# Surplus rows carried into the next table, earlier keys of pairs, and pairs at every second group in a graph-convolution kernel

## The chip, the core and the metric

The kernel runs on one core of a Trainium2 chip, in one launch. The metric is the device time of one execution in microseconds (us), taken over several runs. The core has five engines that work side by side: TensorE (PE, matmuls), VectorE (DVE), ScalarE (ACT), GpSimd (POOL) and SyncE (SP, which here only issues transfers).

## The reference

```python
h = jnp.maximum(_layernorm(x, axis=-1), 0.0)            # x: 12500 nodes x 128
h = h @ W_in2f.T
Wij = smu(f_ij @ W_f1.T + b_f1) @ W_f2.T + b_f2         # f_ij: 400000 edges x 20
Wij = Wij * rcut_ij[:, None]
x_ij = h[idx_j] * Wij                                    # idx_j sorted, idx_i random
agg = jax.ops.segment_sum(x_ij, idx_i, num_segments=12500)
out = x + smu(agg @ W_o1.T + b_o1) @ W_o2.T + b_o2
```

Per edge, a filter of 128 numbers is made from 20 features, multiplied with a row of `h` and added to the row of the edge's source node. The edges lie in the order of `idx_j`, so the rows of `h` are near each other, but the sums go to random nodes. That is what the kernel is built around.

## The kernel before, in words

Edges are worked on in tiles of 128, in groups of 4 tiles (`GRP`) and in sups of 2 groups; there are 3125 tiles, 782 groups and 391 sups. The nodes fall into 98 bins of 128. Each group makes its messages (edges on partitions, 128 numbers and the node's place in its bin: a row of 129 numbers, `ROW`), and POOL scatters them by an indirect transfer into a table in DRAM that has `CAP` slots for each bin. One scatter sends one row from each of 128 partitions, so a group needs four.

The sups are split into ten epochs (`PARTS`; called stages in the prediction). The messages of epoch k are scattered into table k (three stores, taken in turn), and while epoch k+1 is worked on, the table of epoch k is read back (`fetch`, on SP), DVE makes for each tile of 128 rows a selection matrix from the places (`choose`, tile `se`), and PE adds the tile to its bin's sum by a matmul (`add`). A table of 768 slots per bin is 6 tiles per bin, so 588 matmuls. A place carries a mark of its round, so that old rows in a store don't match. Stores that are used for the first time are cleared by transfers of a zero tile (`clear`), spread over the groups of the epoch before.

Which slot a row gets is worked out beforehand: DVE marks the bins of a sup (`mark_bins`), keeps running counts per bin (`bins`), PE makes prefix sums of the marks (`count`), DVE takes each row's slot from PSUM (`read`) and adds the bin's start (`number`).

In some groups rows are paired. In such a group rows of tiles 0 and 1 are matched with rows of tiles 2 and 3 that go to the same bin (`spread_keys`, `match`), rows that found a partner are moved beside it by permuting matmuls (`rank_left`, `place_left`, `permute`, `take_pairs`), and two scatters send two rows from each partition. The rows that found none are collected in one tile of leftovers (`lt`, at most 112 rows), which is counted and scattered with a later group, its host. A pair therefore needs 2 + 1 scatters in place of 4. `EVERY` says after how many groups another one is paired.

The order of the work on PE, DVE, ACT and SP is written out by hand: at step p the loop sends the messages of group p (those of a paired group one step later), numbers, weighs and mixes group p+1, counts and reads group p+2, and marks the bins of group p+3; the sums (`parts`) are spread evenly over an epoch's steps. The 23 sups of the last two epochs are worked early, one after every eight others in epochs 1 to 4; their messages are kept in DRAM and scattered at the end ("kept" groups). POOL's order follows from the calls of `scatter`.

## Time and profile before

| | |
|---|---|
| Time before, median of 3 runs | 3832.49 us (3823.35 to 3832.53) |
| The profiled execution's own time | 3826.85 us |
| Its span, first to last instruction | 3825.1 us |
| Mean granted TensorE clock | 0.964 of full speed |
| Busy share: PE, DVE, ACT, POOL | 86%, 81%, 74%, 75% |
| First and last scatter begin at | 12.99 and 3763.56 us |

The busy share counts the time in which an engine executes something. Time between two instructions in which it only takes up the next one does not count, and an engine can be at its limit with a share well below 100%. "issue" in a list of waits is such time.

### The profile page before, as it was taken

The page shows a single profiled execution, that of the slowest core. Times are in us where ns is not written, and L with a number is a line of the kernel's source. Part 1 is how long each engine was busy: PE and PEld are TensorE (multiplying, and loading weights), DVE is VectorE, ACT ScalarE, POOL GpSimd, SP SyncE. Part 2 cuts the span into 40 slices and gives each one's busy share as a digit, 9 for nine tenths or more (in the row PEclk, how much of TensorE's full clock was granted, in tenths as well). Part 3 has the DMA queues.
Part 4 walks back from the last instruction along what each step waited for, and adds up shares of the span by engine and source line. Part 5 has one row for each costly group of instructions (what it writes and reads, how often), then busy time and mean ns, then how long its engine had stood idle before and what let it go on. Part 6 is the DMA issues. An engine that isn't in the chain of part 4 may idle for free.

```text
span 3825.1 us, 90354 instructions
## 1 busy us (share of the span) xinstructions
PE 3294.2 (86%) x28066; PEld 2872.9 (75%) x28066; DVE 3116.8 (81%) x8275; ACT 2839.2 (74%) x7986; POOL 2855.5 (75%) x2946
## 2 busy tenths in 40 slices
PE   8777776988888999999989889999999889997767
PEld 4346665877777888878878778888888888887657
DVE  7878976877777888888888888888898888886657
ACT  7767766878888888888888888888778777875102
POOL 6777777777767777777777777777777777777776
PEclk9989988999999999999999999999999999999889
DMA  5888888888888878888878878888888888886977
GB/s 156 231 236 239 236 230 233 248 251 246 263 253 232 238 227 231 244 239 235 229 222 232 235 214 242 253 239 247 232 244 249 233 235 246 241 236 177 312 247 228
DMA packets 663936, 905.06 MB, mean 237 GB/s; under 512 B 179875, under 2 KB 462631, under 8 KB 663321
## 3 DMA queue, kind: packets, MB, share of 16 engines
q1 hardware_dynamic: 556025, 666.99, 63.5%
q0 software_dynamic: 100112, 219.93, 17.8%
q10 hardware_dynamic: 7312, 12.29, 0.9%
q8 instruction: 228, 3.74, 0.4%
q14 instruction: 259, 2.12, 0.2%
HBM read 500.66 MB, written 398.23 MB: 235 GB/s over the span
## 4 chain that ended last, share of the span: by engine, by line
PE 33%; DMA 18%; DVE 16%; ACT 11%; issue 11%; POOL 9%; SPq 2%; ACTq 0%; DVEq 0%; POOLq 0%
DMA buf<-ms,ix 12%; PE pg L1168 10%; POOL buf L1110 9%; PE pw L998 6%; PE pt L875 5%; ACT hg L973 3%; PE pc L752 3%; DVE se L1155 3%; DVE mt L838 2%; DVE ms L1040 2%; ACT oh L634 2%; ACT ge L926 2%; PE ph L954 2%; PE pw L1000 1%; DVE pc L796 1%
## 5 line engine op out<-in xcount | busy, mean ns | idle before, releaser
L1110 POOL DMA_INDIRECT buf<-ms,ix x2516 | 2444.3, 971 | 813.6 <-issue 569.0
L1168 PE MATMUL pg<-se,rw 128*128 128x128 f32 x8036 | 1168.7, 284 | 107.8 <-DVE se L1155 61.2
L1168 PEld LDWEIGHTS pg<-se,rw 128*128 128x128 f32 x8036 | 1037.2, 194 | 166.4 <-issue 65.5
L973 ACT ACTIVATE hg<-ph,w_sb 128x128 f32<-128x128 f32 x2784 | 781.9, 361 | 94.5 <-PE ph L954 80.4
L998 PE MATMUL pw<-w_f,ge 128*128 128x128 f32 x5568 | 779.2, 284 | 30.5 <-DVE ms L1040 14.3
L998 PEld LDWEIGHTS pw<-w_f,ge 128*128 128x128 f32 x5568 | 697.5, 197 | 50.0 <-issue 23.7
L1155 DVE TENSOR_TENSOR se<-irow_ps,rw 128x1536 f32<-128x1536 f32 (+1 forms) x345 | 587.4, 1703 | 112.1 <-DMA rw<-buf 89.5
L634 ACT ACTIVATE oh<-rbc,nrow 128x512 bf16<-128x512 uint8 x725 | 538.6, 743 | 33.5 <-DMA rbc<-rel_dram 33.1
L635 ACT ACTIVATE oh<-oh,onesb 128x512 bf16<-128x512 bf16 x743 | 536.0, 721 | 24.2
L796 DVE TENSOR_REDUCE pc<-pc 128x4 f32<-128x392 f32 (+1 forms) x782 | 466.4, 596 | 81.0 <-PE pc L752 77.4
L1040 DVE TENSOR_TENSOR ms<-pw,hg 128x512 f32<-128x512 f32 x482 | 330.2, 685 | 137.8 <-DMA buf<-ms,ix 36.5
L875 PE MATMUL pt<-ms,mt 128*128 128x129 f32 x2676 | 345.0, 279 | 55.0 <-DVE at L855 48.2
L875 PEld LDWEIGHTS pt<-ms,mt 128*128 128x128 f32 x2676 | 319.1, 193 | 66.7 <-issue 23.3
L752 PE MATMUL pc<-eo,tri 128*128 128x392 f16 x782 | 261.5, 334 | 69.8 <-DVE ix L818 46.8
L954 PE MATMUL ph<-hw,oh 126*128 126x128 bf16 x2784 | 274.4, 221 | 39.0 <-ACT hg L973 36.0
L926 ACT ACTIVATE ge<-pu 128x512 f32<-128x512 f32 x451 | 272.9, 605 | 17.4 <-PE pu L918 15.5
L752 PE MATMUL pc<-so,ones_h 128*128 128x392 f16 (+1 forms) x996 | 279.4, 306 | 0.1
L1000 PE MATMUL pw<-wls,f 128*128 128x128 bf16 x2784 | 274.2, 222 | 0.0
L1088 ACT ACTIVATE ms<-lo_b,mark 128x4 f32<-128x4 uint8 x309 | 91.3, 295 | 231.9 <-DVE ms L1040 219.7
L1110 POOL DMA_INDIRECT buf<-lt,ix x214 | 203.3, 950 | 78.0 <-issue 27.7
L954 PEld LDWEIGHTS <-oh 126*128 126x128 bf16 x2784 | 217.0, 99 | 52.5 <-issue 44.3
L752 PEld LDWEIGHTS <-ones_h 128*128 128x128 f16 x1554 | 151.8, 98 | 139.2 <-issue 17.1
(344 smaller groups left out, 5313.0 us busy)
## 6 DMA issues: line engine op xcount, KB each, us to landing
rw<-buf SPq DMA_DIRECT2D x292, 774.0 KB
f<-f_parts SPq DMA_DIRECT2D x370, 240.0 KB
buf<-zero SPq DMA_DIRECT2D x146, 387.0 KB
rbc<-rel_dram SPq DMA_DIRECT2D x389, 128.0 KB
buf<-ms,ix POOLq DMA_INDIRECT x2516
f_parts<-hs SPq DMA_DIRECT2D x105, 360.0 KB
rw<-buf SPq DMA_DIRECT2D x49, 645.0 KB
f_parts<-hs SPq DMA_DIRECT2D x107, 240.0 KB
```

Of the source, the lines that this page charges most:

```text
L634: nc.scalar.activation(oh, loaded[s][1][:, o:o + n], AF.Abs, bias=pneg if s < FEW // SUP else nrow)
L635: nc.scalar.activation(oh, oh, AF.Relu, scale=-1.0, bias=onesb[:, 0:1])
L752: nc.tensor.matmul(to, by, of, start=start, stop=stop, skip_group_check=True)
L796: nc.vector.tensor_reduce(sl[:, :n], pc[:, :n], op=ALU.max, axis=AX.X)
L875: nc.tensor.matmul(po[:, j * (ROW + 1):j * (ROW + 1) + w], pp[:, o:o + P], ms[:, i, ROW:ROW + w], start=(i == 0), stop=(i == 1))
L954: nc.tensor.matmul(ph[:, j * P:(j + 1) * P], oh[:3 * WIN, a:a + P], hw[:3 * WIN, g % PER, :], start=True, stop=True)
L973: nc.scalar.activation(hg[:, j * P:(j + 1) * P], rows_of[g][:, j * P:(j + 1) * P], AF.Copy, scale=w_sb[:, t + j:t + j + 1])
L998: nc.tensor.matmul(pw[:, a:a + P], ge[:, a:a + P], w_f2, start=(a == 0), stop=False, skip_group_check=True)
L1040: nc.vector.tensor_tensor(ms[:, :n, 0:P], pw.rearrange("p (j f) -> p j f", f=P)[:, :n], hg.rearrange("p (j f) -> p j f", f=P)[:, :n], op=A ...
L1110: i = nc.gpsimd.indirect_dma_start(out=(wide if g in host or g in pair_no else bufs)[k][:, :], out_offset=bass.IndirectOffsetOnAxis(ap=ix, ...
L1155: nc.vector.tensor_tensor(se[:, a:a + n], own.unsqueeze(1).to_broadcast([P, n, P]), rows_in[c][:, a:a + n, P:P + 1].to_broadcast([P, n, P] ...
L1168: nc.tensor.matmul(pgs[0][:, g, :], rows_in[c][:, o, 0:P], sel[c][:, o, :], start=(q == 0), stop=(q == Q[k] - 1))
```

## The change

Five things change together:

1. The tables of a chain of epochs lie in one store with `S` slots for each bin, each at its own offset `OFF`. Rows of epoch k that find no slot in table k take the first slots of table k+1, and epoch k+1 begins to count behind them (`carry`). So the tables need less room for chance: five tables of 640 slots per bin in place of four of 768 and one of 640. Only the last of a chain has the room for the worst case. The first chain has five tables, of which none lies where another lay, the second three, and the last two epochs one each; all of these are put over the first chain's tables.
2. Five tables are cleared in place of three, each only above the slots that are sure to be filled, by transfers from 64 partitions; the clearing of table k+1 ends at three quarters of epoch k, since surplus rows may come from then on.
3. The epochs' lengths change and pairs come at every second group in epochs 2, 3 and 4 (the third to fifth pass).
4. The key of a paired group is made one step earlier, right behind its slots, in place of the start of the step that transposes it.
5. The places of the leftovers are subtracted on PE (a matmul of the identity with `spot`, ahead of the two that rank) and not on DVE; and a host's leftovers are marked and added to the count in one operation.

```diff
-PARTS = (59, 58, 58, 58, 47, 37, 27, 24, 16, 7)
-EVERY = (3,) + (2.5,) * 7
-UNPAIRED = 10
+PARTS = (58, 55, 54, 53, 48, 42, 33, 25, 16, 7)
+CHAINS = (5, 3, 1, 1)
+EVERY = 3, 2.5, 2, 2, 2, 2.5, 2.5, 2.5, 2.5
+UNPAIRED = 8
-SIGMA = 4.6
+SIGMA = 4.0
-ZP = 128
+ZP = 64
...
+    for i, n in enumerate(CHAINS):
+        a = len(CAP)
+        ends = [0]
+        for k in reversed(range(a, a + n)):
+            ends.insert(0, max(ends[0] + 1, math.ceil(sum(rows_for(k, a + n)) / P)))
+        caps = [(u - v) * P for u, v in zip(ends, ends[1:])]
...
-    stores = [dram.tile([NB * CAP[k] + SPILLS * SPILL, ROW], F32, name=f"buf{k}") for k in range(min(BUFS, EPOCHS))]
+    store = dram.tile([NB + SPARE, S, ROW], F32, name="buf")
...
             if g in first:
-                nc.vector.memset(before, 0.0)
+                if carried(first[g]):
+                    nc.vector.tensor_scalar(before, carry, BIG, None, op0=ALU.min)
+                else:
+                    nc.vector.memset(before, 0.0)
...
                 if g in host:
-                    lot = cnt.tile([P, NB], F16, name="el")
                     rows_of_bins(k)
-                    nc.vector.tensor_scalar(lot, bin_row, left_of[host[g]][1], None, op0=ALU.is_equal)
-                    nc.vector.tensor_add(then, whole, lot)
+                    lot = then
+                    nc.vector.scalar_tensor_tensor(then, bin_row, left_of[host[g]][1], whole, op0=ALU.is_equal, op1=ALU.add)
...
+                if carried(k + 1):
+                    on_one = bank_of[:, 1, :NB]
+                    nc.tensor.matmul(on_one, one_h, after, start=True, stop=True)
+                    nc.vector.tensor_scalar(carry, on_one, -float(CAP[k]), 0.0, op0=ALU.add, op1=ALU.max)
...
         def rank_left(g):
...
-            nc.tensor.matmul(at_, tri, met_of(g, 0, 2), start=True, stop=False, skip_group_check=True)
+            nc.tensor.matmul(at_, ident, spot, start=True, stop=False, skip_group_check=True)
+            nc.tensor.matmul(at_, tri, met_of(g, 0, 2), start=False, stop=False, skip_group_check=True)
...
         def place_left(g):
-            at_ = cnt.tile([P, 2], F32, name="at")
-            nc.vector.tensor_tensor(at_, spot, kt[:, 2 * P:2 * P + 2], op=ALU.subtract)
             nc.vector.tensor_tensor(pp[:, 4 * P:].rearrange("p (j e) -> p j e", j=2),
-                                    irow_ps.unsqueeze(1).to_broadcast([P, 2, P]),
-                                    at_.unsqueeze(2).to_broadcast([P, 2, P]), op=ALU.is_equal)
+                                    falling.unsqueeze(1).to_broadcast([P, 2, P]),
+                                    kt[:, 2 * P:2 * P + 2].unsqueeze(2).to_broadcast([P, 2, P]), op=ALU.is_equal)
...
         def scatter_rows(g, rows, ix):
+                for j in range(FIRST):
+                    if (j == 0 and g >= BY) or 0 < j <= k or (j == k + 1 and is_clean(g)):
+                        behind_all(i, after_clear[j])
...
-            elif k + 1 < BUFS:
+            elif k + 1 < FIRST and cleared < len(cleans):
                 past = BY if k == 0 else 0
-                upto = min(len(cleans), -(-(i + 1 - past) * len(cleans) // (ng - 4 - past)))
+                upto = min(len(cleans), -(-(i + 1 - past) * len(cleans) // (by_group[k] - g0 - 2 - past)))
...
-            number(at(p + 1))
+            if at(p + 1) not in paired:
+                number(at(p + 1))
...
             read(at(p + 2))
+            if at(p + 2) in paired:
+                number(at(p + 2))
```

`behind_all` makes a scatter wait for the transfers named; `by_group[k]` is the group at three quarters of epoch k.

## Rows read from the trace of the kernel before

**Rows 1.** The page's first part: busy us, share of span, instructions

```profile
PE 3294.2 (86%) x28066; PEld 2872.9 (75%) x28066; DVE 3116.8 (81%) x8275; ACT 2839.2 (74%) x7986; POOL 2855.5 (75%) x2946
```

**Rows 2.** The page's costliest groups: scatters (count; busy us, mean ns; idle before)

```profile
L1110 POOL DMA_INDIRECT buf<-ms,ix x2516 | 2444.3, 971 | 813.6 <-issue 569.0
...
L1110 POOL DMA_INDIRECT buf<-lt,ix x214 | 203.3, 950 | 78.0 <-issue 27.7
```

**Rows 3.** POOL's timeline: start, duration, operation, idle before

```profile
1002.25 1.01 POOL L1110 DMA_INDIRECT buf<-ms,ix  x1 [0.30 <-issue]
```

**Rows 4.** Busy us in stages 1 to 7: PE, PEld, DVE, ACT, POOL; clock, DMA

```profile
596.00:1172.00 576.00, 488.67 (x4238) 433.92 (x4237) 440.99 (x1208) 461.33 (x1317) 414.51 (x428) 0.95 0.87 249
1172.00:1699.00 527.00, 480.33 (x4320) 428.81 (x4319) 450.00 (x1199) 449.95 (x1291) 400.74 (x415) 1.00 0.84 237
1699.00:2246.00 547.00, 491.37 (x4355) 436.58 (x4354) 457.70 (x1225) 467.01 (x1305) 415.30 (x430) 0.99 0.81 230
2246.00:2685.00 439.00, 410.80 (x3701) 371.57 (x3701) 381.85 (x996) 364.64 (x1025) 333.96 (x345) 0.99 0.85 240
2685.00:3025.00 340.00, 317.86 (x2942) 293.49 (x2941) 300.59 (x785) 267.65 (x758) 258.07 (x268) 0.99 0.87 243
3025.00:3290.00 265.00, 241.26 (x2184) 221.31 (x2184) 224.78 (x570) 196.01 (x551) 201.51 (x209) 0.98 0.82 238
3290.00:3504.00 214.00, 198.23 (x1827) 180.42 (x1826) 187.90 (x488) 167.16 (x473) 162.82 (x168) 1.00 0.77 224
```

**Rows 5.** POOL's waits in stage 1: waited for: us, times, longest

```profile
POOL buf L1110 <- ACT ms L1090: 22.7, 14, 5.1
POOL buf L1110 <- DVE ix L821: 14.5, 6, 4.7
```

**Rows 6.** POOL's waits from 1172 to 3504 us, the first of the list

```profile
POOL buf L1110 <- issue: 415.0, 1359, 0.8
```

**Rows 7.** DVE's timeline in stage 2: first and last of 126 slot reads

```profile
1173.68 0.57 DVE L796 TENSOR_REDUCE pc<-pc 128x4 f32<-128x392 f32 x1
...
1687.74 0.57 DVE L796 TENSOR_REDUCE pc<-pc 128x4 f32<-128x392 f32 x1
```

**Rows 8.** PE's timeline: a run of matmuls that sum tiles

```profile
3601.56 2.84 PE L1168 MATMUL pg<-se,rw 128*128 128x128 f32 x24
```

**Rows 9.** Groups by shape: the selects

```profile
L1155 DVE TENSOR_TENSOR se<-irow_ps,rw 128x1536 f32<-128x1536 f32 x292 | 511.0, 1750 | 107.3 <-DMA rw<-buf 87.7 <-PE pg L1168 18.9 <-DMA rbc<-rel_dram 0.3
...
L1155 DVE TENSOR_TENSOR se<-irow_ps,rw 128x1280 f32<-128x1280 f32 x49 | 72.6, 1482 | 4.8 <-PE pg L1168 2.8 <-DMA rw<-buf 1.8
```

**Rows 10.** Waits in stage 3, all engines: DVE for message buffers

```profile
DVE ms L1040 <- DMA buf<-ms,ix: 23.2, 13, 4.7
```

**Rows 11.** Waits in stage 1, all engines: sums and table rows

```profile
PE pg L1168 <- ACT agg L1180: 16.4, 11, 3.2
...
DVE se L1155 <- DMA rw<-buf: 13.2, 2, 8.6
```

**Rows 12.** Waits over the whole span: for the key and for `at`

```profile
PE pt L830 <- DVE key L812: 70.9, 63, 6.3
...
PE pt L875 <- DVE at L855: 48.2, 47, 2.3
```

**Rows 13.** Groups by shape: what a pair adds on DVE

```profile
L838 DVE SCALAR_TENSOR_TENSOR mt<-pt,key,onesb 128x256 f32<-128x256 f32 x428 | 189.4, 480 | 13.7 <-PE pt L830 12.9 <-DVE ms L1031 0.2
...
L856 DVE TENSOR_TENSOR mt<-irow_ps,at 128x256 f32<-128x256 f32 x223 | 94.7, 424 | 7.7
...
L724 DVE TENSOR_SCALAR el<-mv,lat 128x98 f16<-128x98 f32 x214 | 65.5, 306 | 0.3
...
L855 DVE TENSOR_TENSOR at<-spot,pt 128x2 f32<-128x2 f32 x214 | 32.0, 150 | 4.6 <-PE pt L849 4.0
```

**Rows 14.** Groups by shape: a pair's small matmuls and its transposes on PE

```profile
L830 PE MATMUL pt<-ident,key 128*128 128x128 f32 x428 | 85.9, 283 | 77.2 <-DVE key L812 70.9 <-ACT hg L973 1.8 <-ACT ed L661 1.3
...
L848 PE MATMUL pt<-met,tri 128*128 128x2 f16 x192 | 32.1, 167 | 27.0 <-DVE mt L838 25.3
```

More of the change, by code (lines that the diff above doesn't have):

```diff
@@ L112, in gnn_kernel, with rows_for @@
-    assert all(c <= CAP[k % BUFS] for k, c in enumerate(CAP)) and (EPOCHS - 1) // BUFS < GRP
+    def rows_for(a, b):
+        n = sum(n for _, n in eps_of[a:b])
+        extra = WIDER * sum(PAIRS[a:b]) / (SUP // GRP)
+        per = SUP * P * P / N
+        return (n + extra) * per, SIGMA * math.sqrt((n + 2 * extra) * per)
+    CAP, OFF, LIM, ZMIN, chain_of = [], [], [], [], []
+    assert sum(CHAINS) == EPOCHS
+    for i, n in enumerate(CHAINS):
[4 more added lines that the diff above has]
+        caps = [(u - v) * P for u, v in zip(ends, ends[1:])]
+        at_ = 0 if i <= 1 else OFF[-1] + CAP[-1]
+        for j, c in enumerate(caps):
+            CAP.append(c)
+            OFF.append(at_ + sum(caps[:j]))
+            LIM.append(c + (caps[j + 1] if j + 1 < n else 0))
+            chain_of.append(i)
+            less = eps_of[a + j][1] * SUP * P * P / N - rows_for(a + j, a + j + 1)[1]
+            ZMIN.append(max(0, math.floor(less / ZP) * ZP) if i == 0 else 0)
@@ L113, in gnn_kernel @@
+    FIRST = CHAINS[0]
+    S = OFF[FIRST - 1] + CAP[FIRST - 1]
+    assert all(o + c <= OFF[FIRST - 2] for o, c in zip(OFF[FIRST:], CAP[FIRST:]))
     Q = [c // P for c in CAP]
-    ROWS = 2 * max(Q)
+    ROWS = max(2 * max(Q), 3 * GRP)
     SPAN = [ROWS // q for q in Q]
-    assert all(NB * c + P + max(CAP) + 2 * int(BIG) < NOBIN_ROW and c < BIG - 1 for c in CAP)
+    SPILL = P + int(BIG) + max(LIM)
+    SPILLS = 3
+    SPARE = -(-(SPILLS * SPILL + S) // S)
+    assert (NB + SPARE) * S + 2 * int(BIG) < NOBIN_ROW and all(n < BIG - 1 for n in LIM)
@@ L208, in gnn_kernel @@
     spot = const.tile([P, 2], F32, name="spot")
+    falling = const.tile([P, P], F16, name="falling")
+    one_h = const.tile([P, P], F16, name="one_h")
+    carry = const.tile([P, NB], F16, name="carry")
     drow = const.tile([P, SPILLS * EPOCHS], F32, name="drow")
     CB = 2
-    zero = const.tile([ZP, CB * max(c - z for c, z in zip(CAP[:BUFS], ZMIN)) * ROW // ZP], F32, name="zero")
+    zero = const.tile([P, CB * 3 * ROW], F32, name="zero")
     cleans = [(b, n) for b, n in chunks(NB - 1, CB)] + [(NB - 1, 1)]
@@ L563, in gnn_kernel @@
         pair_no = {g: i for i, g in enumerate(list(paired) + late_pairs)}
+        assert all(sum(epoch[g // PER] == k for g in pair_no) <= n for k, n in enumerate(PAIRS))
         more_met = down.bitcast(F16)
@@ L767, in count @@
                     part(pc[:, n], tri, lot)
[L768 removed]
+                    part(pc[:, n], rest_h, since[:, 2], stop=True)
             counts[g] = pc, sl
@@ L1109, in scatter_rows @@
                 k = epoch[g // PER]
[L1110 to L1120 removed]
+                i = nc.gpsimd.indirect_dma_start(out=rows_at, out_offset=bass.IndirectOffsetOnAxis(ap=ix, axis=0),
+                                                 in_=rows, in_offset=None)
@@ new lines, in scatter_rows @@
+                sent[k].append(i.ins.name)
+                for j in range(k + 1):
+                    apart(i, f"slots{j}")
+                apart(i, "fetched")
+                tc.add_to_no_dep_group(f"slots{k}", i.ins)
+                for j in range(FIRST):
+                    if (j == 0 and g >= BY) or 0 < j <= k or (j == k + 1 and is_clean(g)):
+                        behind_all(i, after_clear[j])
+                    else:
+                        apart(i, f"cleared{j}")
+                if k == FIRST:
+                    for j in range(FIRST - 2):
+                        behind_all(i, after_fetch[j])
@@ new lines, in gnn_kernel, with is_clean, behind_all, apart @@
+        sent = [[] for _ in range(EPOCHS)]
+        after_clear = [[] for _ in range(FIRST)]
+        after_fetch = [[] for _ in range(EPOCHS)]
+        def is_clean(g):
+            k = epoch[g // PER]
+            return k + 1 < FIRST and g > by_group[k]
+        def behind_all(i, names):
+            for name in names:
+                tc.add_manual_dep(i.ins, name, AFTER, reason="rows of a table")
+            names.clear()
+        def apart(i, others):
+            tc.declare_no_dep(i.ins, group=others, reason="slots are disjoint")
@@ new lines, in fetched, with cleared_rows @@
+        def fetched(i, k):
+            behind_all(i, sent[k])
+            for j in range(k + 1, EPOCHS):
+                apart(i, f"slots{j}")
+            tc.add_to_no_dep_group("fetched", i.ins)
+            after_fetch[k].append(i.ins.name)
+        def cleared_rows(k, c):
+            for i in clear(k, c, nc.sync):
+                for j in range(EPOCHS):
+                    apart(i, f"slots{j}")
+                tc.add_to_no_dep_group(f"cleared{k}", i.ins)
+                after_clear[k].append(i.ins.name)
@@ L1122, in gnn_kernel @@
+        by_group = {k: eps_of[k][0] * PER + eps_of[k][1] * PER * 3 // 4 for k in range(FIRST - 1)}
+        clean_by = set(by_group.values())
         rows_in, sel, pgs = {}, {}, {}
```

134 lines of the change are left out of this document (57 added, 77 removed).

## The prediction

> **What bounds the kernel now.** I read the page's first lines, then the costliest groups, then POOL's own timeline, then all engines stage by stage, and last who waits for whom.
>
> By busy share PE leads with 86% and POOL stands at 75% [rows 1]. The reader should not stop there. POOL's scatters cost 0.971 us each when they carry messages and 0.950 us when they carry pair leftovers [rows 2], and on the timeline each is followed by 0.30 us in which POOL waits for nothing but its next instruction [rows 3]. So one scatter takes 1.273 us, and the count of scatters is fixed by the loop: 2902 (3125 tiles less one for each of 223 pairs). 2902 x 1.273 = 3694 us of a span of 3825.1. What is left is the start, the tail after the last scatter, and stalls.
>
> Where are the stalls? I call the epochs stages 0 to 9 and cut them where DVE closes each. Stage 1 has 576 us [rows 4] and 427 scatters (4 x 116 groups, less 37 pairs): 543.6 us, so 32 us stalled; POOL's wait list names what it waited for there, ACT's `places_in` and DVE's number of a leftover [rows 5]. From 1172 to 3504 the longest entry of the same list is the gap between scatters, and none of its 1359 gaps is over 0.8 us [rows 6]: stages 2 to 7 together took 2332 us and their 1850 scatters need 2355. So from stage 2 on POOL sets the pace, in stage 1 the other engines do. Stage 0 has its own stalls at the start; I leave them as they are.
>
> How much room the other engines have matters as much. Stage 2 took 527 us on DVE's clock while its 429 scatters need 546 us: the others run 3.5% faster than POOL there. In stage 4 (439 us against 347 x 1.273 = 442) the two are equal, and in stage 6 (265 against 252) POOL lives from messages made earlier. Kernel time is a race of two nearly equal runners.
>
> To forecast the second runner I write a stage's own time as 2.95 us per step (a group, kept ones too) + 0.17 us per 128-row tile summed + 1.4 us per pair. The pair price is a least-squares fit of step lengths between DVE's slot reads (126 steps of stage 2, [rows 7], give 1.6 +- 0.35 us; stage 4 gives 1.4 +- 0.45). The tile price lies between 0 and 0.37 us (24 matmul records, that is 12 tiles, in 2.84 us are 0.237 each on PE [rows 8], and 1.75 us of DVE select for 12 tiles 0.146 [rows 9]); 0.17 is where the other stages agree. The step price is then solved from stage 2: 128 steps, 588 tiles, 35 pairs, 527 us. It gives 441 for stage 4 (measured 439), 338 for stage 5 (340), 213 for stage 7 (214); for stage 6 it is 14 low. For stage 3 it gives 533 against 547, but there DVE waited 23 us for message buffers that POOL had not freed [rows 10], so POOL sets that stage. Stage 1 comes out at 529 against 576: a surcharge of 46 us, which I take to be ACT copying that stage's sums (PE waits 16.4 us for it there [rows 11]).
>
> **The change, part by part.**
>
> *More pairs, other stage lengths.* The loop now places 250 pairs and 9 late ones, so 2866 scatters: 72 message scatters less and 36 leftovers more, 72 x 1.273 - 36 x 1.252 = 46.6 us of POOL, back to back, on the path. By stage 1 to 4 POOL needs 404, 388, 381, 346 scatters = 514, 494, 485, 440 us.
>
> *Smaller tables.* Surplus rows go to the next table, so tables 0 to 3 have 5 tiles per bin for 6: 392 matmuls less of 4116 and 196 selects of 1.750 us become 1.482 us, 52.5 us of DVE [rows 9]. Both engines are off POOL's path, so this counts only in the second runner: 490 summed tiles per stage for 588, 0.17 x 98 = 17 us in each of stages 1 to 4.
>
> *Early keys, and the leftover's place made on PE.* PE waited 70.9 us for the key and 48.2 us for `at` in the whole run [rows 12], about 0.5 us per pair. One DVE operation of 150 ns goes, and `el` (306 ns) with the addition behind it becomes one operation, taken as 306 [rows 13]: the addition goes, a small f16 one that I put at 0.2, so about 0.35 us of DVE per pair. Against it stands a new matmul of `ident` with two columns. No row shows one in f32; the nearest, two columns in f16, takes 167 ns, and two whole f32 transposes take some 0.4 us (283 ns each, overlapped) [rows 14]. I take 0.2, the nearer row. It waits for nothing, so it is issued while DVE still matches (2 x 0.48 us [rows 13]); without that cover it would cost up to 0.4 us for each of 125 pairs in stages 2 to 4, 50 us of PE. I take 1.0 us for a new pair, with 0.6 and 1.4 as ends.
>
> *Carry and flags.* Each of 6 hand-overs between tables adds a matmul and a DVE operation, four more flags as much again: about 0.5 us of latency each, 5 us at the most, inside the second runner. ACT's places lose their bias in stages 3 and 4; I count nothing for it.
>
> *Clears.* Five tables of about 10 MB are cleared (97 bins x 192 rows x 516 B, table 4 with 256 rows), for three of 19.6. Stage 1 halves, stages 2 and 3 get 9.9 and 13.1 MB that they had not, against 6.5 MB less of fetches each. They are issued by the third quarter of the stage before, and POOL must wait for them at the first scatter after it, with two groups of margin (9 us) and the lead. Behind a wait there stand all later scatters. I count nothing: a clear reads a constant tile, so SP waits for no engine before it, and three such tables are cleared under stages 0 and 1 now.
> The new clears read the zero tile from 64 partitions. [...]
>
> *The race after the change.* Second runner, with 1.0 us a pair: stage 1 (122 steps, 490 tiles, 36 pairs) 479 + 46 = 525 us against POOL's 514; stage 2 (120, 490, 44) 481 against 494; stage 3 (117, 490, 43) 472 against 485; stage 4 (107, 490, 38) 437 against 440; stages 5, 6 and 7 361, 284 and 215 against 390, 307 and 233. So 11 us of stall in stage 1, and for stages 2 to 4, where the margin falls from 19 us to 13, 13 and 3, I allow 8 us. Stages 8, 9 and the tail are not touched.
>
> **Sum.** -46.6 (scatters) - 32 (stall of stage 1 now) + 11 + 8 = -59.6 us. The profiled execution took 3826.85 us (span 3825.1 and 1.75 around it), so 3767; the median of the runs shown is 5.6 above the profiled one, which lies inside their 3823 to 3833. I say 3770.
>
> Ends: stage 1 without stall and pairs at 0.6 us leave nothing to add, 3826.85 - 78.6 = 3748. The upper end is the first rival.
>
> **Rivals.**
>
> *The other engines become the bound in stages 1 to 4.* If a pair costs the whole of its DVE work (2 x 480 + 424 + 150 + 306 ns, 1.84 us [rows 13], taken as 2.5 with some four small operations beside them) and nothing gets cheaper, the step price solved from stage 2 is 2.65 us and stages 1 to 4 need 541, 512, 501 and 462 us: stalls of 26, 18, 16 and 22. The sum is -46.6 - 32 + 82 = +4, 3831 us, no change. For it: DVE is busy 85% of stage 2 and PE 91% [rows 4]. Against it: the fits, and the waits on key and `at` that go. Chance 0.13.
>
> *The clears slow stages 2 and 3; this one ends slower.* Suppose the 46 us surcharge of stage 1 is not ACT's but that of its 19.6 MB of clears, 2.35 us per MB. By bytes alone stage 1 gets 23 us back and stages 2 and 3 take 23 and 31, which ends at 3784, inside my range. [...] It ends slower than before from about 4.0 us per MB on. [...] Against it: the list of waits in stage 1 blames ACT, and a wait for a table's rows stands behind ACT's in that list [rows 11]. Chance 0.05.
>
> *The scatters themselves grow dearer*, by waits on the clears or by one store in place of three. 0.021 us each would eat the gain (2866 x 0.021 = 60, 3827 us). Against it: the two kinds of scatter, into the table alone and with its overflow, differ by 0.02 us only [rows 2]. Chance 0.04.
>
> *Better than forecast*: no stall in stages 1 to 4, 3748. Chance 0.06.
>
> **The numbers.** The forecast has 0.72 with an own range of 3750 to 3792. With 0.06 at 3748 and 0.22 between 3827 and 3849, I reach below to 3743 and above to 3815, where the forecast and the first rival mix (a pair at about 2 us); that leaves out some 0.18. A difference under 0.3% (11.5 us, the runs shown differ by 9) can't be told from none. Faster by more than that: 0.72 + 0.06 and half of the first and third rival, 0.86. Within it: the rest of these two, 0.08. Slower: the second rival and 0.01 of the first, 0.06.
>
> **What would show it.** 2866 scatters, still 1.27 us apart; POOL without waits from stage 2 on; stage 1 about 50 us shorter. The group that matches keys without a wait of PE for a key. Selects of 1280 columns and none of 1536. Wrong: POOL waits of tens of us in stages 2 to 4 on ACT's `places_in` or the leftover's number (first rival), on clears (second), or a longer scatter (third).

## The result and the profile after

The kernel after takes 3835.68 us (median of 20 runs, 3826.65 to 3843.70), the kernel before 3828.74 beside it (20 runs). The ratio is 1.0018, 95% interval 1.001 to 1.0025: slower by 0.2%, within the 0.3% that the prediction takes for no difference, where 3770 was forecast. The profiled execution took 3838.41 us, its span is 3836.5. In ten of the eighteen runs told below, the kernel before itself took 5639 to 5714 us, so every ratio is to the kernel before as it ran beside that run.

The page of the kernel after, busy share and scatters (answers to [rows 1, 2]):

```profile
PE 3315.9 (86%) x28144; PEld 2916.9 (76%) x28458; DVE 3070.7 (80%) x8104; ACT 2838.8 (74%) x8132; POOL 2837.5 (74%) x2911
...
L1133 POOL DMA_INDIRECT buf<-ms,ix x2444 | 2388.4, 977 | 833.6 <-issue 532.1
...
L1133 POOL DMA_INDIRECT buf<-lt,ix x250 | 239.8, 959 | 88.1 <-issue 24.7
```

The count is as forecast: 72 scatters of messages fewer, 36 of leftovers more, 2866 in all. POOL's busy time fell by 18 us, and yet the span grew by 11.4. So POOL waits more, and the windows of stages 1 to 4 say where to look (answer to [rows 4]; busy us of PE, PEld, DVE, ACT, POOL, then clock, DMA share, GB/s):

```profile
581.00:1106.00 525.00, 456.97 (x3946) 407.09 (x3998) 404.51 (x1090) 438.18 (x1256) 399.45 (x413) 0.96 0.85 237
1106.00:1627.00 521.00, 467.73 (x4159) 422.50 (x4212) 427.08 (x1148) 429.57 (x1257) 384.83 (x396) 0.98 0.85 238
1627.00:2153.00 526.00, 462.64 (x4071) 417.89 (x4123) 417.11 (x1117) 413.44 (x1211) 363.98 (x375) 0.96 0.85 234
2153.00:2604.00 451.00, 420.82 (x3799) 379.88 (x3846) 391.38 (x1040) 383.64 (x1119) 343.13 (x351) 1.00 0.81 231
```

Stage 1 came out at the forecast 525, but by luck: that was the other engines' time, with POOL stalled for 11 us, and what took 525 us is POOL itself, without a stall (412 scatters x 1.273 = 524). Stages 2 and 3 were to take POOL's 494 and 485 and took 521 and 526. POOL's waits in stage 3 of the kernel after (waited for: us, times, longest), where before only the gap between scatters stood at the head of the list [rows 6]:

```profile
POOL buf L1133 <- issue: 85.1, 248, 4.0
POOL buf L1133 <- ACT lt L926: 17.8, 4, 6.3
POOL buf L1133 <- ACT ms L1113: 15.3, 9, 3.1
POOL buf L1133 <- DVE ix L849: 11.9, 12, 6.0
```

The names are those of the work that ends last in a group: the copy of the leftovers' tile (`lt`), the messages' places, the leftover's number. The table sums, from POOL's timeline, the idle time before each scatter over the usual 0.305 us; I call it stall. The last eight columns are experiments, told below under the names in the second row.

| POOL's stall, us | before | after | after, again | every 2.5 | clears in stages 0, 1 | ends' matmul early | mended | 128 partitions | clears twice | before, denser pairs |
|---|---|---|---|---|---|---|---|---|---|---|
| run | | | g1_control | g2_every25 | g3_clears_sooner | g4_spot_early | h1_mended | h2_clear128 | h3_clears_twice | h4_before_pairs |
| stage 0 | 26.9 | 36.6 | 39.7 | 39.7 | 62.8 | 39.6 | 25.7 | 25.3 | 39.7 | 25.9 |
| stage 1 | 31.6 | 0.3 | 0.2 | 0.2 | 71.2 | 0.2 | 3.1 | 1.2 | 0.2 | 25.0 |
| stage 2 | 0.3 | 16.1 | 13.1 | 0.2 | 25.9 | 8.7 | 22.8 | 22.9 | 48.9 | 29.4 |
| stage 3 | 1.0 | 48.0 | 45.6 | 13.1 | 8.4 | 40.9 | 20.9 | 24.4 | 114.3 | 4.3 |
| stage 4 | 0.3 | 1.1 | 2.3 | 0.2 | 2.3 | 2.3 | 3.6 | 2.3 | 2.4 | 23.9 |
| scatters | 2902 | 2866 | 2866 | 2895 | 2866 | 2866 | 2876 | 2866 | 2866 | 2872 |
| span | 3825.1 | 3836.5 | 3835.4 | 3823.6 | 3895.7 | 3817.5 | 3811.6 | 3803.5 | 3930.4 | 3838.2 |

Groups by shape of the kernel after (answers to [rows 9, 12, 14]):

```profile
L1214 DVE TENSOR_TENSOR se<-irow_ps,rw 128x1280 f32<-128x1280 f32 x245 | 363.3, 1483 | 47.5 <-DMA rw<-buf 23.4 <-PE pg L1227 21.4 <-DMA f<-f_parts 2.1
...
L858 PE MATMUL pt<-ident,key 128*128 128x128 f32 x500 | 98.8, 280 | 26.1 <-DVE key L840 21.0 <-ACT lt L926 3.1 <-ACT ed L671 1.4
L876 PE MATMUL pt<-spot,ident 128*128 128x2 f32 x500 | 86.6, 243 | 75.3 <-DVE mt L866 73.4
L876 PEld LDWEIGHTS pt<-spot,ident 128*128 128x128 f32 x500 | 77.9, 196 | 103.0 <-DVE mt L866 97.4 <-issue 3.9
...
L1214 DVE TENSOR_TENSOR se<-irow_ps,rw 128x1536 f32<-128x1536 f32 x96 | 168.1, 1751 | 84.3 <-DMA rw<-buf 81.1 <-PE pg L1227 3.0
```

The early keys work: PE's wait for them falls from 70.9 to 21.0 us. But the new matmul of `ident` and `spot`, two records for each pair (500 for 250 pairs), is where PE now waits for DVE's match. One such place in stage 3, in the timeline of the kernel after (start, duration, engine, operation, idle before):

```profile
1667.22 1.41 SPq L237 DMA_DIRECT2D buf<-zero  x2
1668.73 2.61 SPq L1712 DMA_DIRECT2D f_parts<-hs  x3
1671.39 1.32 SPq L237 DMA_DIRECT2D buf<-zero  x2
1673.03 1.07 SPq L1200 DMA_DIRECT2D rw<-buf  x1
...
1680.69 1.49 DVE L1214 TENSOR_TENSOR se<-irow_ps,rw 128x1280 f32<-128x1280 f32 x1 [11.10 <-DMA rw<-buf]
...
1683.30 0.47 DVE L866 SCALAR_TENSOR_TENSOR mt<-pt,key,onesb 128x256 f32<-128x256 f32 x1
...
1684.11 0.08 DVE L866 DVE_READ_ACCUMULATOR mt<-pt,key,onesb 128x1 f16 x1
1684.24 0.59 PE L876 MATMUL pt<-spot,ident 128*128 128x2 f32 x2 [12.66 <-DVE mt L866]
...
1689.57 0.96 POOL L1133 DMA_INDIRECT buf<-ms,ix  x1 [2.83 <-issue]
```

Read it downwards. SP issues four clears (L237) and three stores, then a load of table rows at 1673.03. DVE's next select has to wait for such a load for 11.1 us, until 1680.69. The match stands behind the select in DVE's order, PE has gone as far as the new matmul and idles 12.7 us, and POOL, which was still living from finished messages, runs dry at 1689.57. With a lead such loads cost POOL little (58 us of waits for loads with 13.1 us of stalls in stage 3 of `g2_every25`, below); here there is none.

### The profile page after: what moved, and what is told of

The parts are those of the page before. It is cut to its first block, busy times and chain, and to the rows that moved or that the text cites. A ratio compares the mean times of both kernels' runs of the same rounds, so it can differ in the third digit from the quotient of the medians.

```text
span 3836.5 us, 90850 instructions
## 1 busy us (share of the span) xinstructions
PE 3315.9 (86%) x28144; PEld 2916.9 (76%) x28458; DVE 3070.7 (80%) x8104; ACT 2838.8 (74%) x8132; POOL 2837.5 (74%) x2911
## 4 chain that ended last, share of the span: by engine, by line
PE 38%; DVE 15%; DMA 14%; issue 8%; ACT 8%; POOL 6%; SPq 2%; ACTq 0%; DVEq 0%; POOLq 0%; another core or an unknown queue 0%
PE pg L1227 10%; DMA buf<-ms,ix 9%; PE pw L1025 8%; PE pt L902 7%; POOL buf L1133 6%; PE pc L767 4%; ACT hg L1000 3%; DVE mt L866 2%; PE ph L981 2%; PE pw L1027 2%; DVE se L1214 2%; DVE pc L824 1%; DVE ms L1053 1%; DMA rbc<-rel_dram 1%; DVE ms L1063 1%
## 5 line engine op out<-in xcount | busy, mean ns | idle before, releaser
L1133 POOL DMA_INDIRECT buf<-ms,ix x2444 | 2388.4, 977 | 833.6 <-issue 532.1
L1227 PE MATMUL pg<-se,rw 128*128 128x128 f32 x7252 | 1080.2, 284 | 107.5 <-DVE se L1214 63.1
L1227 PEld LDWEIGHTS pg<-se,rw 128*128 128x128 f32 x7252 | 946.5, 194 | 152.9 <-issue 57.0
L1214 DVE TENSOR_TENSOR se<-irow_ps,rw 128x1280 f32<-128x1280 f32 (+1 forms) x345 | 535.2, 1551 | 132.0 <-DMA rw<-buf 104.5
L902 PE MATMUL pt<-ms,mt 128*128 128x129 f32 (+1 forms) x3108 | 415.0, 285 | 55.3 <-DVE mt L883 23.1
L902 PEld LDWEIGHTS pt<-ms,mt 128*128 128x128 f32 x3108 | 384.4, 199 | 69.7 <-issue 27.6
L1133 POOL DMA_INDIRECT buf<-lt,ix x250 | 239.8, 959 | 88.1 <-issue 24.7
L767 PE MATMUL pc<-so,ones_h 128*128 128x392 f16 x782 | 260.8, 333 | 0.0
L866 DVE SCALAR_TENSOR_TENSOR mt<-pt,key,onesb 128x256 f32<-128x256 f32 x500 | 220.2, 477 | 13.7 <-PE pt L858 13.2
L1027 PEld LDWEIGHTS <-f 128*128 128x128 bf16 x2784 | 221.1, 100 | 9.6
```

Source lines behind the costliest of these rows:

```text
L767: nc.tensor.matmul(to, by, of, start=start, stop=stop, skip_group_check=True)
L902: nc.tensor.matmul(po[:, j * (ROW + 1):j * (ROW + 1) + w], pp[:, o:o + P], ms[:, i, ROW:ROW + w], start=(i == 0), stop=(i == 1))
L1027: nc.tensor.matmul(pw[:, a:a + P], fb[:, o + a:o + a + P], wls, start=False, stop=(a + P == n), skip_group_check=True)
L1133: i = nc.gpsimd.indirect_dma_start(out=rows_at, out_offset=bass.IndirectOffsetOnAxis(ap=ix, axis=0), in_=rows, in_offset=None)
L1214: nc.vector.tensor_tensor(se[:, a:a + n], own.unsqueeze(1).to_broadcast([P, n, P]), rows_in[c][:, a:a + n, P:P + 1].to_broadcast([P, n, P] ...
L1227: nc.tensor.matmul(pgs[0][:, g, :], rows_in[c][:, o, 0:P], sel[c][:, o, :], start=(q == 0), stop=(q == Q[k] - 1))
```

## The experiments

The runs named g and h come first; the kernel before took 3823.66 us beside the g runs and 3824.74 beside the h runs. The ten named e, f and i come last. An expectation names the theories that it sets against each other by letters.

**The kernel after again.** No edit; the reference for the three runs below.

> The changed kernel itself, unaltered, as the control beside the three that follow. On a chip like that of the first two profiles: ratio to before 1.000 to 1.004, POOL's stalls of stages 2 and 3 at 50 to 75 us. On a chip where the engines wait longer for each other's signals (as in the runs e and f) every theory expects it slower than before by more, 1.006 to 1.013, since a pair adds a chain of hand-overs between PE and DVE.

Measured: 3833.86 us, ratio 1.0021 (1.0006 to 1.0037). The stalls of the table repeat within 4 us.

**Pairs at every 2.5 groups in stages 2 to 4**, as the kernel before has them:

```diff
-EVERY = 3, 2.5, 2, 2, 2, 2.5, 2.5, 2.5
+EVERY = 3, 2.5, 2.5, 2.5, 2.5, 2.5, 2.5, 2.5
```

> The changed kernel with pairs after 2.5 groups in all stages (29 pairs less, 2895 scatters). Against the control of the same call. Theory B (too many pairs for DVE, PE and ACT in stages 2 and 3): the stalls of stages 2 and 3 all but vanish, 27 us faster than the control or more. Theory A (the matmul of `spot`): 29 pairs at half a microsecond, 15 us of stalls less against 37 us more of scatters, 15 to 25 us slower. Theory C (clears in stages 2 and 3): 30 to 40 us slower than the control.

Measured: 3818.77 us, 0.9985 (0.9976 to 0.9995). 29 scatters more, 37 us of POOL, and still some 15 us faster than the control: the stalls of stages 2 and 3 fall from 58.7 to 13.3 us. That is theory B, with half of its 27 us. The last pairs cost more than they save. The clears are all there, and PE, DVE and ACT wait even longer for loads in stage 3, 58 us in place of the control's 37. With fewer pairs the same kind of late load hardly reaches POOL.

**Clears moved from stages 2 and 3 into 0 and 1** (tables 1 and 2 are cleared in stage 0, tables 3 and 4 in stage 1):

```diff
-            elif k + 1 < FIRST and cleared < len(cleans):
+            elif k < 2:
...
+                lot = [(2 * k + j, c) for j in (1, 2) for c in range(len(cleans))]
```

> The changed kernel with the clears of tables 1 and 2 in stage 0 and those of tables 3 and 4 in stage 1. Against the control of the same call. Theory C: waits for loads in stages 2 and 3 below 5 us, POOL's stalls there under 20 us, 20 to 45 us faster. Theories A and B: within 10 us.

Measured: 3892.20 us, 1.0176 (1.0162 to 1.0189), 58 us above the control, where theory C had 20 to 45 below. Stage 3 loses its stalls (45.6 to 8.4), as theory C said, but stages 0 and 1 gain 23 and 71 us. The waits of stage 0 in this kernel name the loads:

```profile
ACT oh L644 <- DMA rbc<-rel_dram: 74.4, 18, 9.1
...
PE pu L945 <- DMA f<-f_parts: 40.9, 11, 8.6
POOL buf L1133 <- ACT ms L1113: 30.5, 16, 6.8
```

In both stages where the clears were put, loads come late and POOL stalls. Stage 2, which has no clears here, stalls for 25.9 us all the same: its stalls have another cause. Stage 3's stalls shrink without clears there (8.4) and shrink with fewer pairs (13.1 in the run above), so there it takes both.

**The matmul of the ends ahead of the match**, with the transposes of the keys:

```diff
                 nc.tensor.transpose(kt[:, j * P:(j + 1) * P], keys_of[g][:, j:j + 1].to_broadcast([P, P]), ident)
+            nc.tensor.matmul(kt[:, 2 * P:2 * P + 2], ident, spot, start=True, stop=False, skip_group_check=True)
...
-            nc.tensor.matmul(at_, ident, spot, start=True, stop=False, skip_group_check=True)
```

> The changed kernel with the matmul of `spot` ahead of the match. Against the control of the same call. Theory A: 25 to 50 us faster. Theories B and C: within 10 us.

Measured: 3824.51 us, 1.0006 (0.9997 to 1.0015), 9 us below the control; the intervals overlap a little. The stalls fall by 9.5 us, where theory A had 25 us or more. PE's wait in front of the matmul is gone (in the control it was 72.6 us):

```profile
L859 PE MATMUL pt<-spot,ident 128*128 128x2 f32 x500 | 71.6, 213 | 0.0
```

**Clears from 128 partitions**, with as many rows or more (the expectation takes the bytes for the same, but four of the five tables get a third more):

```diff
-ZP = 64
+ZP = 128
```

> The clears are read from 128 partitions instead of 64, the same bytes. Theory P (the source on 64 partitions is what slows the loads): the loads' waits of the third and fourth stage (10 and 37 us in the control) fall by half or more, stalls fall by 20 us or more, ratio about 0.996 to 0.998. Theory Q (the bytes and the place in the queue are what slows them): stalls as in the control within 10 us, ratio 1.001 to 1.005. On the other chip the same edit was slower than the others beside it by about 0.2%.

Measured: 3803.11 us, 0.9942 (0.9927 to 0.9957): 30 us below the control (whose kernel before took 1 us less) and 0.6% faster than the kernel before; theory P had 0.996 to 0.998. The queue of SP's transfers (packets, MB, share of 16 engines' time), over the whole span of the control and of this run:

```profile
q1 hardware_dynamic: 558649, 635.23, 61.5%
```

```profile
q1 hardware_dynamic: 582713, 648.04, 62.5%
```

12.8 MB more are moved (the first slot that is cleared is rounded down to a multiple of 128), in more packets, in less time. Stage 3 takes 500 us for 525 and stage 0 569 for 583; stages 1, 2 and 4 stay within some 5 us. ACT's wait for `rbc` in stage 3, in the control and in this run:

```profile
ACT oh L644 <- DMA rbc<-rel_dram: 11.8, 8, 3.2
```

```profile
ACT oh L644 <- DMA rbc<-rel_dram: 2.7, 1, 2.7
```

Stage 3, where both runs clear the same rows, has the same queue at (control, then this run):

```profile
q1 hardware_dynamic: 75363, 89.42, 65.0%
```

```profile
q1 hardware_dynamic: 74453, 89.24, 65.5%
```

That is 341 us of all 16 engines for 525 us of stage, and 328 us for 500: 13 us less for the packets. The clears issued on SP also get fewer and cheaper, as the list of line L237 shows for the control and for this run (duration in ns, least, median, most):

```profile
L237 SPq DMA_DIRECT2D buf<-zero x301: 522/655/2423, 47.6 to 2025.2; - x151
```

```profile
L237 SPq DMA_DIRECT2D buf<-zero x249: 377/451/3275, 47.1 to 1994.4; - x125
```

Summed over the trace, that is 215 us of SP's time against 162, and loads stand in the same queue. By stages neither difference fits alone as the reason. In stage 3 half as many clears are issued (50 for 99) and SP's time for them falls from 69 to 33 us; PE, DVE and ACT wait 15 us for loads in place of 37. In stage 0 as many are issued (99 for 100), SP's time hardly falls (73 to 67 us), 6 MB more are moved, and still the waits for loads fall from 28 to 2 us. In stages 1 and 2, with as many clears and more bytes, they don't fall (13 to 16 us, 10 to 20).

**Clears of tables 3 and 4 issued twice**, the second time into rows that nobody reads:

```diff
+            if k >= 3:
...
+                rows = junk[k - 3, b:b + n, z:CAP[k], :].rearrange("b (p s) r -> p b (s r)", p=ZP)
+                for o, w in chunks(m, zero.shape[1] // n):
+                    nc.sync.dma_start(rows[:, :, o:o + w], zero[:ZP, :n * w].rearrange("p (b m) -> p b m", b=n))
             for i in clear(k, c, nc.sync):
```

> The clears of tables 3 and 4 (in the third and fourth stage) are issued twice, the second time into rows that nobody reads: 13.1 MB more in each of the two stages. Theory Q (the clears' bytes delay the loads): the waits for loads in the two stages rise by 40 us or more together, stalls by 40 to 80 us, 3875 to 3915, ratio 1.012 to 1.022. Theory M (the margin that the pairs took is the cause, the clears only stand beside it): stalls rise by 0 to 15 us, ratio 1.002 to 1.006.

Measured: 3937.90 us, 1.0302 (1.0285 to 1.0319), more than either theory gave. Stage 3 takes 592 us, 67 more than the control, stage 2 takes 35 more. (Table 3 has 9.9 MB of clears, table 4 13.1, so stage 2 got 9.9 MB more, and not the 13.1 of the expectation.) ACT's wait in stage 3, and the added clears on SP:

```profile
ACT oh L645 <- DMA rbc<-rel_dram: 100.6, 26, 11.5
```

```profile
L1180 SPq DMA_DIRECT2D junk<-zero x150: 515/653/1336, 1120.9 to 2128.9; - x150
```

The same wait was 11.8 us with the clears issued once. So clears that nobody waits for do delay the stage. They can do it by their place in SP's queue or by the DMA engines' time. The added issues take 35 us of SP's time in stage 2 (51 of them) and 67 in stage 3 (99), just what the stages grew by. But the DMA engines also take some 40 and 60 us more, all 16 together (a share of 0.87 of 552 us and 0.86 of 592, for 0.85 of 516 and of 525 in the control), which is not far from it, so this run does not part the two.

**The kernel before with the denser pairs and nothing else of the change** (the second line keeps its tables at 768 rows):

```diff
-EVERY = (3,) + (2.5,) * 7
+EVERY = (3, 2.5, 2, 2, 2, 2.5, 2.5, 2.5)
-SIGMA = 4.6
+SIGMA = 4.2
```

> The kernel before with pairs at every second group in the third to fifth pass and nothing else of the change, but for its bound on the sizes (so that its tables stay at 768 rows): 2872 scatters, 28 fewer, and no clears in the third to fifth stage. Theory Q (the clears cause the stalls there): POOL doesn't wait in those stages for more than 10 us, and the time falls by 28 x 1.273 = 36 us, to 3790 to 3800, ratio 0.990 to 0.993. Theory M (the pairs at every second group take the margin by themselves): stalls of 30 us or more in these stages and a ratio of 0.998 or above.

Measured: 3844.09 us, 1.0059 (1.004 to 1.0077), slower than before with 30 scatters fewer, as theory M had it. Stages 2 to 4 of this run:

```profile
1163.00:1713.00 550.00, 501.22 (x4457) 452.08 (x4515) 470.51 (x1296) 459.11 (x1334) 396.22 (x409) 0.99 0.79 228
1713.00:2260.00 547.00, 500.31 (x4492) 450.67 (x4550) 478.64 (x1323) 474.91 (x1349) 413.28 (x426) 1.00 0.80 232
2260.00:2709.00 449.00, 418.14 (x3791) 381.78 (x3839) 397.15 (x1065) 371.25 (x1057) 323.72 (x334) 1.00 0.81 236
```

No table is cleared in these stages, and the engines wait for loads for 0.5 us in stage 2. Against [rows 4] it takes 550 us for 527 and stage 4 takes 449 for 439, with 11 and 8 pairs more (46 for 35, 37 for 29, from the records of the match, four to a pair). POOL waits for the others in both stages now, and before it was behind them in stage 2 and level with them in stage 4. So I read the growth as the pairs' price (stage 3 is left out, since POOL set it before): 33 us for 19 pairs, 1.74 us each (2.1 in stage 2, 1.25 in stage 4). POOL's waits in stage 2 of this run:

```profile
POOL buf L1110 <- issue: 89.6, 294, 0.3
POOL buf L1110 <- DVE ix L821: 16.3, 11, 5.7
POOL buf L1110 <- ACT ms L1090: 10.9, 14, 1.9
POOL buf L1110 <- ACT lt L899: 8.3, 4, 4.5
```

They are the names of stage 3 of the kernel after, with no clears beside them.

**Mended: ends' matmul early, 2.5 in stage 3, clears spread to 7/8 of an epoch.**

```diff
-EVERY = 3, 2.5, 2, 2, 2, 2.5, 2.5, 2.5
+EVERY = 3, 2.5, 2, 2.5, 2, 2.5, 2.5, 2.5
-eps_of[k][0] * PER + eps_of[k][1] * PER * 3 // 4
+eps_of[k][0] * PER + eps_of[k][1] * PER * 7 // 8
```

> The kernel after with three edits: the matmul of the ends issued with the transposes ahead of the match, pairs at every 2.5 groups in the fourth stage (2 in the third and fifth as it was), and each stage's clears spread to 7/8 of its last epoch instead of 3/4. 2876 scatters instead of 2866: 10 x 1.273 = 13 us more. Theory A (the fourth stage's stalls are work of PE and DVE over the margin, made late by clears): the stalls of 46 us there go, those of the third stage shrink by a few us: 3833 + 13 - 46 - 5 = about 3795 to 3805, ratio 0.992 to 0.996 to the kernel before. Theory B (the stalls come from something else, such as the order of loads, which follows the scatters about): 3825 to 3840, ratio 1.000 to 1.004.

Measured: 3820.49 us, 0.9997 (0.9985 to 1.0009), between the two theories' times. Stage 3's stalls are halved and stage 2's are not; with 64 partitions for the clears it does not beat before. Stage 0 has 14 us of stalls less than in the control. The early matmul alone left it at 39.6, and the pairs were changed in stage 3 only, so that is the wider spread of the clears.

**The runs with long hand-offs.** e3_every25 is the same code as g2_every25 above. Its waits over the whole span:

```profile
POOL buf L1133 <- DVE ix L849: 856.3, 172, 10.9
ACT hg L1000 <- remote: 632.2, 152, 12.8
...
PE pt L876 <- DVE mt L866: 357.6, 108, 8.2
```

POOL is busy 50% of that span, for 75% of the other, and the mean granted clock is 0.818 for 0.959. Here the chain of hand-offs sets the time and not POOL's scatters, so these ten runs tell what an edit adds to that chain. Why hand-offs took longer no run tells.

`e1_at_dve` puts the subtraction of the leftovers' places back on DVE; `e2` and `f4` are the early ends' matmul, `e3` pairs at every 2.5, `e4` 128 partitions, `f1` the clears in stages 0 and 1, `f3` the clears twice. `f2` issues the clears of tables 1 to 4 (stages 0 to 3) on ACT's queue. `i1` halves the clears of the run with 128 partitions (493 on SP's queue for 249), and `i2` joins 128 partitions, the early ends' matmul and pairs at every 2.5 in stages 2 and 3:

```diff
-            nc.tensor.matmul(at_, ident, spot, start=True, stop=False, skip_group_check=True)
...
+            nc.vector.tensor_tensor(at_, spot, kt[:, 2 * P:2 * P + 2], op=ALU.subtract)
```

```diff
-            for i in clear(k, c, nc.sync):
+            for i in clear(k, c, nc.sync if k == 0 else nc.scalar):
```

```diff
-        for o, w in chunks(m, zero.shape[1] // n):
+        for o, w in chunks(m, zero.shape[1] // n // 2):
```

> The changed kernel with one part undone: the leftovers' places are subtracted on DVE again, and PE has no matmul of the identity with `spot`. Theory A (the new matmul stands in PE's queue behind DVE's match, 175 us of PE idle time in front of it in the changed kernel, so each pair costs the other engines more, not less): the 64 us of POOL stalls in stages 2 and 3 fall below 25, ratio to before 0.990 to 0.994. Theory B (pairs at every second group are too many for DVE, PE and ACT whatever this matmul costs): stalls stay within 15 us of 64, ratio 0.999 to 1.003. Theory C (the clears from 64 partitions that now run in stages 2 and 3): as B, 1.000 to 1.003.

> The changed kernel with one matmul moved: the identity with `spot` is issued right behind the two transposes of the keys, ahead of the match, where it has nothing to wait for but PE. Theory A: the wait in front of it goes, stalls of stages 2 and 3 below 25 us, ratio 0.989 to 0.994, at least as good as with the subtraction on DVE. Theory B: 0.999 to 1.003. Theory C: 1.000 to 1.003.

> The changed kernel with pairs after 2.5 groups in all stages: 29 pairs less, so 2895 scatters, 37 us more of POOL. Theory A: each pair less saves half a microsecond or so of PE, stalls fall by half, ratio 1.001 to 1.005. Theory B: the stalls of stages 2 and 3 (64 us) all but vanish, -64 + 37, ratio 0.993 to 0.997. Theory C: stalls stay at about 64 us, ratio 1.008 to 1.013.

> The changed kernel with its tables cleared from 128 partitions (and from slot 384 on in all five, a third more bytes for four of them). [...] Theories A and B: as the changed kernel, 1.000 to 1.004.

> The changed kernel with the clears of tables 1 and 2 issued in stage 0 and those of tables 3 and 4 in stage 1, none in stages 2 and 3. Theory C (the clears stand in SP's queue and on the DMA engines ahead of the loads; in the changed kernel PE, DVE and ACT wait 13.8 and 38.2 us for loads in stages 2 and 3, and 2.8 in stage 4, which has none): such waits fall below 5 us in stages 2 and 3, POOL's stalls there from 64 to under 20 us, and stages 0 and 1 give some 15 us back; ratio to before 0.990 to 0.997. Theory A (the matmul of `spot`) and theory B (too many pairs): stalls of stages 2 and 3 stay at 50 us or more, ratio 1.001 to 1.006.

> The changed kernel with the clears of tables 1 to 4 issued on ACT's queue, not on SP's, where the loads stand. The bytes and their time are the same. Theory C, if the loads wait behind clears in SP's own queue: the waits for loads fall, stalls of stages 2 and 3 under 35 us, less what 250 issues cost ACT, ratio 0.993 to 0.999. Theory C, if it is the DMA engines' time that is shared: no gain, 1.001 to 1.005. Theories A and B: 1.002 to 1.006.

> The changed kernel in which each clear of tables 3 and 4 (stages 2 and 3) is issued twice, once into a DRAM tensor that nothing reads: 23 MB more of the suspected cost, nothing else. Theory C: waits for loads in stages 2 and 3 rise from 52 to 100 us or more, POOL's stalls by 30 to 80 us, ratio 1.009 to 1.023. Theories A and B: within 10 us of the changed kernel, 1.000 to 1.004.

> The changed kernel with the matmul of the identity with `spot` issued right behind the transposes of the keys, ahead of the match (as e2, on a chip whose engines do not wait for each other so long). Theory A: the stalls of stages 2 and 3 fall from 64 us under 30, ratio 0.991 to 0.996. Theories B and C: 0.999 to 1.003.

> The clears are read from 128 partitions, and each is cut into two of half the width: the same bytes as in h2_clear128, at least as many clears on SP's queue as the control's 301. Theory P (the source on 64 partitions slows the transfers): near h2_clear128, ratio 0.993 to 0.997. Theory R (the number of clears, through the time that SP takes to issue each, slows the loads queued behind them): near the control, ratio 1.000 to 1.005.

> The kernel after with clears read from 128 partitions, the matmul of the ends issued with the transposes ahead of the match, and pairs at every 2.5 groups in the third and fourth stage (2 in the fifth as it was). Some 20 scatters more than the kernel after, 25 us. Theory A (the stalls that are left in these stages, 23 and 24 us in h2_clear128, come from the margin that the denser pairs take): they go, and h2_clear128's 3803 + 25 - 45 = about 3783, ratio 0.988 to 0.992. Theory B (they have another cause, such as the order of loads at the stages' ends): they stay, 3815 to 3830, ratio 0.997 to 1.001.

| run | us | ratio, 95% interval |
|---|---|---|
| e1_at_dve | 5744.98 | 1.0062 (1.0044 to 1.008) |
| e2_spot_early | 5756.93 | 1.0073 (1.0052 to 1.0094) |
| e3_every25 | 5724.92 | 1.0005 (0.9983 to 1.0026) |
| e4_clear128 | 5775.52 | 1.0092 (1.0066 to 1.0117) |
| f1_clears_sooner | 5702.70 | 1.011 (1.0075 to 1.0145) |
| f2_clears_on_act | 5740.61 | 1.0164 (1.0119 to 1.021) |
| f3_clears_twice | 5750.08 | 1.0184 (1.0149 to 1.0219) |
| f4_spot_early | 5707.79 | 1.0122 (1.0087 to 1.0157) |
| i1_128_small | 5713.67 | 1.0102 (1.0062 to 1.0141) |
| i2_128_mended | 5648.23 | 0.9994 (0.9967 to 1.0021) |

Eight of the ten ratios lie outside every range that was forecast for them; `f3` lies in theory C's and `i2` in theory B's, which proves little where the kernel is bound by something else. Two things can be said. The two runs with fewer pairs are the only ones level with before; all others are 0.6% to 1.8% slower, which suggests that a pair's work is part of that chain too (the kernel after itself was not run beside them). And the question of `i1` stays open: 128 partitions gained nothing where hand-offs are long (`e4` is no better than `e1` and `e2` beside it), so that `i1` stands level with `e4` tells neither for the transfers' own time nor for the number of clears.

## Why the prediction was wrong

The sum, term by term, from the two profiled executions:

| term | forecast, us | measured, us |
|---|---|---|
| fewer scatters | -46.6 | -30.0 (durations 2814.8 to 2796.2, usual gaps 884.4 to 873.0) |
| stage 1's stalls | -32 + 11 | -31.3 (31.6 to 0.3) |
| stalls of stages 2 to 4 | +8 | +63.6 (1.6 to 65.2) |
| stall of stage 0 | 0 | +9.7 (26.9 to 36.6) |
| start, tail, the rest | 0 | -0.6 |
| sum | -59.6 | +11.4 |

**What held.** POOL's scatters bound the kernel before from stage 2 on, and 2866 of them came. Stage 1 lost its stalls. The wait for keys went. So the gain was there, some 61 us in two terms, and was given back later, in stages 2 and 3.

**"Second runner, with 1.0 us a pair" failed.** I took 1.0 us with ends at 0.6 and 1.4 for a pair's cost on the other engines. The denser pairs alone, in the kernel before, cost 1.74 us each. That is the first rival's place; it took 2.5. With 1.74 us for every pair the step price, solved again from stage 2 of the kernel before, is 2.86 us, and stage 2 comes to 120 x 2.86 + 490 x 0.17 + 44 x 1.74 = 503 us against POOL's 494; 521 was measured. So the race that POOL was to win by 13 us in stage 2 is lost, and 18 us of that stage are still without a price. Taking the pairs back in stages 2 to 4 made the kernel faster, though POOL then has 37 us more to do. The first rival's mechanism is shown; its chance of 0.13 was too low. Its 3831 us is near by luck, since it had stalls of 26, 18, 16 and 22 us in stages 1 to 4, and 0.3, 16.1, 48.0 and 1.1 came.

**"Clears: I count nothing" failed.** Its cover was that SP waits for no engine before a clear. That holds (in the trace of the kernel after, no clear waits more than 0.15 us for anything), and no scatter waited for a clear either. It was the wrong place to look: a clear stands in SP's queue ahead of loads and takes the DMA engines' time (in the timeline above SP issues four clears from 1667.22 us on and then the load at 1673.03, and DVE waits 11.1 us for such a load; the clears issued twice took some 40 and 60 us more of all 16 engines), and the loads are what comes late. Clears from 128 partitions give 21 us of stalls back in stage 3 and 14 in stage 0, clears issued twice take 69 and 36 in stages 3 and 2. Stage 0, whose stalls I left as they are, got 9.7 us of stalls, which go again with 128 partitions or with the clears spread wider. In stage 2 the 128 partitions give nothing back (22.9 us for 13.1), and the stalls there stay without any clears. So the second rival named a mechanism that at the change's own dose is shown for stage 3 alone, and there only together with the denser pairs. The 3849 us at the upper end of the rivals' times take each byte cleared from 64 partitions at twice the 2.35 us per MB, and no run shows that price: 13.1 MB of clears at twice the time would differ by some 48 us of packets' time in stage 3 (an estimate from 328 us for 89.2 MB), and 13 us were measured between 64 and 128 partitions.

**"Which I take to be ACT copying that stage's sums" failed too.** The surcharge of stage 1 of the kernel before was most likely its clears', though no run takes them out of that stage there. The waits of PE, DVE and ACT for loads sum to 48 us in that stage before, to 10 us after with half the clears, and to 120 us with the clears of tables 3 and 4 put there. ACT's copies are still in that stage after, and PE still waits 14.0 us for them where it waited 16.4 [rows 11], without a stall of POOL. I had set that price, 2.35 us per MB, as a rival only.

**"It waits for nothing, so it is issued while DVE still matches" failed.** PE idles 73.4 us in front of it for the match; the matmul that stood in that place in the kernel before had 25.3 us [rows 14]. (The 175 us in an expectation above adds the weight loads' idle time to PE's own.) The matmul uses nothing that the match makes, and yet in the timeline above it begins at 1684.24, just after the match's last record ends at 1684.19. It is a wait in the program: in the trace its weight load idles for 12.81 us until this last record, and the matmul with `tri` behind it, which does need the match, has no wait of its own. It writes into the tile `kt` that the match reads, and stands behind the match in the program; issued ahead of it, it waits for nothing (0.0 us). Which of its neighbours the wait was set for no run tells. The cost was low too: 86.6 us of PE for 250 pairs are 0.35 us each where I took 0.2, nearer to the other row that I had, two transposes. The lost cover is worth about 9 us, by the run with the matmul moved ahead.

**Scatters.** A scatter lasts 0.9757 us on the mean of all (0.9754 in the control) for 0.9699, so some 17 us less are gained than the sum has; the experiments lie between 0.971 and 0.975. About 7 us of it are in stage 0 (0.994 for 0.978). No run tells its cause. The third rival, the dearer scatter, had asked for 0.021 us.

**Not forecast well, without weight.** Selects of 1536 columns were to vanish; 96 of them stay. They are those of the later tables, which have four tiles per bin or fewer and are read 12 tiles at a time, before as after.

**What stays open.** Whether 64 partitions hurt by the transfers' own time (341 us of packets for 328 in stage 3) or by SP's dearer and more numerous issues (655 ns for 451 in the median, 301 for 249); whether a clear delays loads by its place in SP's queue or by the DMA engines' time (the run with the clears on ACT's queue, `f2`, was made only among long hand-offs); and what the version with all mends takes where before takes 3825 us. It too ran only there.

## What to carry to other kernels

When two engines run within a few per cent of each other, price the slower path's added work from a run, not from a fit: the last pairs used up a forecast margin of 13 us and turned 29 saved scatters into a loss. A transfer that nobody waits for was not free here (99 clears more took 67 us of a stage): ask which loads stand behind it in its queue, and whether the consumer has a lead at that moment. Where a constant is written out by transfers, try it from all 128 partitions first; here that edit gained the most, 0.8% of the kernel after, and with it the kernel was 0.6% faster than before.

## What the runs showed of the hardware

Transfers that nothing waits for were not free: with the DMA engines busy 85% of a stage, 99 clears of 13.1 MB more lengthened it by 67 us, and 51 of 9.9 MB another stage by 35 us. That is 5.1 and 3.5 us per MB, but 0.68 and 0.69 us per clear, with a clear's issue on SP at 0.65 us in the median. Late loads by themselves did not set the time: in stage 3, 58 us of waits for loads went with 13 us of POOL's stalls where pairs came at every 2.5 groups, and 37 us of waits with 46 us of stalls where they came at every second.
